# A macaron block on one core: the shared expert taken for two groups of tokens at once, in the two halves of the array's rows

## The chip, the core and the metric

The kernel runs on one core of one Trainium2 chip. The core has a matrix engine (TensorE, "PE" in the profile, with its weight loads shown apart as "PEld"), a vector engine (VectorE, "DVE"), a scalar engine (ScalarE, "ACT"), a general engine (GpSimd, "POOL") and an engine that issues most transfers (SyncE, "SP"). Matrix products are written to PSUM, a small memory of eight banks; one bank holds 128 rows of 512 numbers in float32. VectorE and ScalarE read results out of PSUM; GpSimd works on the larger on-chip memory, SBUF, alone. Each engine runs its own list of instructions in order, and engines wait for each other by semaphores.

The metric is the time of the kernel on the device in microseconds (us), as the median of several runs.

## What is computed

The input x is 8 sequences of 1024 tokens of width 128, all in float32. Three layers follow one another, each on a normalised x (mean and variance over the width of 128):

```python
x = x + 0.5 * ffn(layernorm(x))
x = x + attention(layernorm(x))     # one head of width 128, rotary positions, causal
x = x + 0.5 * ffn(layernorm(x))     # the same weights again
```

The feed-forward layer is a mixture of 16 experts of 64 hidden units, of which each token uses 4, and one shared expert of 64 hidden units that every token uses:

```python
scores = sigmoid(xt @ gate_w.T)                  # 16 scores per token
_, idx = top_k(scores + gate_b, 4)               # the 4 best experts
w = 2.5 * scores[idx] / sum(scores[idx])         # their weights, 0 for the others
y = sum over e of  w[e] * (silu(xt @ gate[e].T) * (xt @ up[e].T)) @ down[e].T
y = y + (silu(xt @ gate_sh.T) * (xt @ up_sh.T)) @ down_sh.T
```

## The kernel before

**Groups and slots.** A feed-forward layer is done in groups of 512 tokens (half a sequence); over the two layers there are 32 groups, numbered p = 0 to 31, in one order that lets attention of the sequences between the layers be filled in. The kernel computes all 16 experts for all tokens: their 1024 hidden units are 8 blocks of 128. A group has an "up" half, slots U0 to U8, and a "down" half, slots D0 to D8. In `up(k)` (line 278) TensorE makes two products of 128x512, gate and up, for block k into two PSUM banks (banks 1 and 0 for even k, 3 and 2 for odd k); ScalarE applies silu to the gate (line 286) and VectorE multiplies (line 288). In `weigh(k)` (line 290) GpSimd multiplies the block by the tokens' expert weights, which were spread over the partitions by a round trip through DRAM (`spread`, line 248). In `down(k)` (line 294) TensorE sums the eight blocks' products in bank 0. After each of these steps, `run(p, slot)` issues whatever other work has been given to that slot.

**The shared expert.** It has 64 gate units and 64 up units, so one product of 128x512 makes both halves (`up_shared_a`, line 267, into bank 5). `up_shared_b` applies silu to the gate half (line 275) and multiplies it by the up half (line 276) into rows 64 to 127 of a tile whose rows 0 to 63 are zero (`shared`, lines 129 to 133; the weights `wsd` have zeros in the same rows). A ninth product, `down(8)`, then adds it to bank 0 as a full product of 128 rows, of which half are zero. It closes the sum; VectorE copies the result out of bank 0 (`yT`, line 306). The shared product of a group is issued at its start, ahead of slot U0, and `down(8)` ahead of slot D8.

**The other work, by slot.** A list `jobs` is filled by hand-written tables of slots. For group p, the work that prepares it is placed in the groups before it: normalisation (`norm_a`, `norm_b`), the transposition into `hT` (`turn`, line 189), the scores of the 16 experts (`route_a`, `route_b`, `score`), the choice of the best four (`top_a` and `top_b` in slot D8, `top_c` in U1, all VectorE), and `spread` in U3. `add` (line 323) turns the previous group's `yT` back and adds it to x in slot U3. Attention is done in queries of 128 tokens: `scores`, `exp`, `turn` (transposing the probabilities), `attend` (line 435). Each group carries two or three queries; their slots are at lines 483 to 487: the first one's `attend` is in D7, the second's first `turn` is in D8, its second in U0 and its `attend` in U2, and a third's turns are in U3 and U4. The projections for a new sequence (`project`, line 361, banks 5 and 4) are in U3 and U4.

**Spare banks.** Everything that is neither up, down, shared, projection nor scores takes its PSUM bank from `other_bank()` (line 73): banks 6 and 7 in turn. An instruction that takes such a bank waits until the last user's result has been read out of it.

**One matmul, two instructions.** A float32 product appears in the profile as two weight loads and two matmuls (two passes), so a line called 256 times shows 512 matmuls. The routing product (line 197) is split over four blocks of 32 columns of the array (`tile_position=(0, j * SW)`), four tiles of 128 tokens each.

**The opening.** For group 0 all preparation runs ahead of the loop: `turn`, `route_a`, `up_shared_a`, `route_b`, `score` and the choice of experts (lines 569 to 580). Slot U1 of group 0 begins with its `spread` (lines 582 to 585), then statistics, a load of x, and the loads of the attention's weights. Groups 1 and 2 have their own tables of places (lines 526 to 531).

Of the kernel before, what the change touches and what calls it, by code (L numbers as in the profile page):

```python
# [26 lines left out]
def kernel(  # L27
# [43 lines left out]
    spare = [0]  # L71

    def other_bank():
        spare[0] += 1
        return bank(6 + spare[0] % 2)
# [51 lines left out]
    nc.gpsimd.memset(wsd[:I, :], 0.0)  # L127
    nc.sync.dma_start(out=wsd[I:, :], in_=w_sh_down)
    shared = []
    for n in range(2):  # L130
        sh = const.tile([P, W], F32, name=f"shared{n}")
        nc.gpsimd.memset(sh[:I, :], 0.0)
        shared.append(sh)
# [43 lines left out]
    class Group:  # L177
# [89 lines left out]
        def up_shared_a(self):  # L267
            self.hidT = big.tile([P, NP, W], F32, tag="hidT", name=f"hidT_{self.nm}")
            self.sh = shared[self.n % 2]
            nc.tensor.matmul(bank(5), ws, self.hT, start=True, stop=True)  # L270

        def up_shared_b(self):
            s_ps = bank(5)
            ss = work.tile([P, W], F32, tag="sg", name=f"ss_{self.nm}")
            nc.scalar.activation(ss[I:, :], s_ps[:I, :], AF.Silu)  # L275
            nc.vector.tensor_tensor(self.sh[I:, :], s_ps[I:, :], ss[I:, :], ALU.mult)

        def up(self, k):

            nm = f"{self.nm}_{k}"  # L280
            units = slice(k * P, (k + 1) * P)
            g_ps, u_ps = bank(2 * (k % 2) + 1), bank(2 * (k % 2))
            nc.tensor.matmul(g_ps, wg[:, units], self.hT, start=True, stop=True)  # L283
            nc.tensor.matmul(u_ps, wu[:, units], self.hT, start=True, stop=True)  # L284
# [3 lines left out]
            nc.vector.tensor_tensor(hid, u_ps, sg, ALU.mult)  # L288
# [5 lines left out]
        def down(self, k):  # L294
            if k == 0:
                self.y = bank(0)
            w, h = (wd[:, k, :], self.hidT[:, k, :]) if k < NP else (wsd, self.sh)
            nc.tensor.matmul(self.y, w, h, start=(k == 0), stop=(k == NP))  # L298
            if k == NP:
                self.yT = work.tile([P, W], F32, tag="yT", name=f"yT_{self.nm}", bufs=2)  # L300
                if self.n == NPER - 1:
                    H = W // 2
                    nc.scalar.copy(self.yT[:, :H], self.y[:, :H])
                    nc.vector.tensor_copy(self.yT[:, H:], self.y[:, H:])
                else:
                    nc.vector.tensor_copy(self.yT, self.y)
# [16 lines left out]
        def add(self):  # L323
# [8 lines left out]
            if self.layer == 1:  # L332
                nc.sync.dma_start(
                    out=out[self.b].rearrange("(t p) d -> p t d", p=P)[:, tiles, :], in_=xg
                )

# [161 lines left out]
    for b in range(B):  # L498
# [5 lines left out]
        else:  # L504
            p0, p1 = st - 2, st - 1
            places = ("D0", "D3", "D5", "D8", "U1", "U3", "U4", "U6")
# [9 lines left out]
        at(st, "U3", lambda h=h: h.project(0, 1))  # L516
        at(st, "U4", lambda h=h: h.project(1, 1))
# [3 lines left out]
    for p, gr in enumerate(groups):  # L521
# [36 lines left out]
    at(0, "U7", lambda: stats("f0_1", 1, range(GT)))  # L558
# [6 lines left out]
    def run(p, slot):  # L565
# [9 lines left out]
    gr.up_shared_a()  # L575
# [6 lines left out]
    jobs[0, "U1"] = [  # L582
        lambda: gr0.spread(4), lambda: stats("f0_0", 0, range(GT, NT)), groups[1].norm_a,
        lambda: load_x(1, 1), load_attention,
    ] + jobs.get((0, "U1"), [])
    gr0 = gr
    for p, gr in enumerate(groups):
        if p > 0:
            gr.up_shared_a()
        gr.up_shared_b()  # L590
        run(p, "U0")
        for k in range(NP):
            gr.up(k)
            if p == 0 and k == 0:
                run(p, f"U{k + 1}")
                gr.weigh(k)
# [3 lines left out]
        for k in range(NP + 1):  # L600
            gr.down(k)
# [76 lines left out]
```

## Time and profile before

| What | Value |
|---|---|
| Median of 3 runs | 1007.22 us (1007.2 to 1007.79) |
| The profiled execution | 1008.41 us, of which 1006.6 us from the first to the last instruction |
| TensorE matmul busy | 988.0 us (98% of the span), 3590 instructions |
| VectorE busy | 663.9 us (66%) |
| ScalarE busy | 427.4 us (42%) |
| GpSimd busy | 451.8 us (45%) |
| Granted TensorE clock, mean | 0.998 of full speed |
| Shared expert's product up (line 270) | 32 products, 32.8 us busy |
| Shared expert's product down (line 298, `wsd`) | 32 products, 33.0 us busy |

The profile is of one execution. Busy time of TensorE is from the start of a matmul to its modelled end, and consecutive matmuls overlap; so what a product costs is read from the distance between its start and the next one's start. The idle time before an instruction and what ended it are given in brackets in the profile. A wait of the matrix engine is often shown at its weight load, which waits on the semaphore, and only in part at the matmul that follows it.

### The profile page before, as it was taken

What the parts mean: (1) busy time and instruction counts of PE and PEld (TensorE: products, weight loads), DVE (VectorE), ACT (ScalarE), POOL (GpSimd) and SP (SyncE); (2) the same over time, 40 slices, a digit from 0 to 9 for tenths busy, and PEclk for the clock granted to TensorE, in tenths of its full rate; (3) what the DMA queues carried; (4) which work ended last, traced back from release to release, by engine and by line L of the source; (5) the groups of instructions that cost most, each with busy time, mean ns of one, the idle gap of its engine ahead of it and who ended that gap; (6) DMA issues with size and microseconds to landing.
All of it is one profiled execution on the core that took longest, in us unless ns stands there. A gap on an engine that the chain in (4) does not pass through costs nothing.

```text
span 1006.6 us, 11516 instructions
## 1 busy us (share of the span) xinstructions
PE 988.0 (98%) x3590; PEld 516.4 (51%) x3590; DVE 663.9 (66%) x2034; ACT 427.4 (42%) x767; POOL 451.8 (45%) x382
## 2 busy tenths in 40 slices
PE   8999999999999999999999999999999999999998
PEld 5444445554555555545554555545554555455443
DVE  5766877668766667666767656776667757665542
ACT  3334435443544444443544444444444444343321
POOL 2445556244633464234634455234653355322434
PEclk9999999999999999999999999999999999999999
DMA  5645343044303532145403452134422243224440
GB/s 164 167 106 105 86 85 84 3 105 85 85 13 83 117 85 51 35 95 117 86 15 76 90 117 68 29 74 96 95 53 59 60 95 87 47 59 95 96 96 21
DMA packets 56830, 80.23 MB, mean 80 GB/s; under 512 B 3584, under 2 KB 23360, under 8 KB 56640
## 3 DMA queue, kind: packets, MB, share of 16 engines
q1 hardware_dynamic: 55488, 78.23, 34.7%
q10 hardware_dynamic: 1280, 1.26, 0.4%
q8 instruction: 28, 0.46, 0.2%
q14 instruction: 34, 0.28, 0.1%
HBM read 74.24 MB, written 5.24 MB: 79 GB/s over the span
## 4 chain that ended last, share of the span: by engine, by line
PE 89%; DVE 7%; issue 2%; ACT 1%; POOL 0%; ACTq 0%; POOLq 0%; DVEq 0%
PE psum L298 24%; PE psum L283 19%; PE psum L284 19%; PE psum L400 6%; PE psum L439 6%; PE psum L427 3%; PE psum L367 3%; PE psum L270 2%; PE psum L172 2%; DVE hidT L288 2%; PE psum L381 1%; DVE sel L237 1%; PE psum L197 1%; PE psum L328 1%; PE psum L139 1%
## 5 line engine op out<-in xcount | busy, mean ns | idle before, releaser
L292 POOL TENSOR_TENSOR hidT<-hidT,cb 128x512 f32<-128x512 f32 x256 | 323.8, 1271 | 515.7 <-DVE hidT L288 484.1
L284 PE MATMUL psum<-hT,wu 128*128 128x512 f32 x512 | 261.5, 592 | 0.6 <-DVE hidT L288 0.6
L283 PE MATMUL psum<-hT,wg 128*128 128x512 f32 x512 | 261.8, 593 | 0.0
L286 ACT ACTIVATE sg<-psum 128x512 f32<-128x512 f32 x256 | 152.7, 597 | 229.4 <-PE psum L283 216.5
L298 PE MATMUL psum<-hidT,wd 128*128 128x512 f32 x512 | 247.5, 601 | 0.0
L288 DVE TENSOR_TENSOR hidT<-psum,sg 128x512 f32<-128x512 f32 x256 | 175.4, 686 | 96.8 <-PE psum L284 93.8
L284 PEld LDWEIGHTS psum<-hT,wu 128*128 128x128 f32 x512 | 97.2, 190 | 123.4 <-issue 103.0
L298 PEld LDWEIGHTS psum<-hidT,wd 128*128 128x128 f32 x512 | 90.1, 191 | 80.9 <-issue 74.1
L283 PEld LDWEIGHTS psum<-hT,wg 128*128 128x128 f32 x512 | 88.5, 191 | 64.2 <-issue 61.6
L439 PEld LDWEIGHTS psum<-v,prT 128*128 128x128 f32 x576 | 74.4, 192 | 30.6 <-issue 26.3
L431 ACT COPY prT<-psum 128x512 f32<-128x512 f32 (+2 forms) x64 | 32.4, 506 | 108.1 <-PE psum L427 107.4
L439 PE MATMUL psum<-v,prT 128*128 128x128 f32 x576 | 74.6, 275 | 0.0
L400 PE MATMUL psum<-k,q 128*128 128x512 f32 (+2 forms) x192 | 72.4, 486 | 0.0
L443 DVE SCALAR_TENSOR_TENSOR x<-psum,rl,x 128x128 f32<-128x128 f32 x64 | 22.1, 346 | 68.3 <-PE psum L439 38.9
L163 DVE TENSOR_SCALAR xn_f<-x,mv_f,rs_f 128x128 f32<-128x128 f32 x128 | 64.9, 567 | 1.2 <-POOL rs_f L156 1.2
L427 PEld LDWEIGHTS psum<-ident,pr 128*128 128x128 f32 x288 | 36.7, 141 | 50.2 <-issue 34.2
L400 PEld LDWEIGHTS psum<-k,q 128*128 128x128 f32 x192 | 36.5, 190 | 45.9 <-issue 45.2
L406 DVE TENSOR_REDUCE top<-psum 128x1 f32<-128x128 f32 (+3 forms) x64 | 48.5, 758 | 2.2
L427 PE MATMUL psum<-ident,pr 128*128 128x128 f32 x288 | 47.4, 274 | 1.9 <-DVE x L331 1.9
L411 ACT ACTIVATE pr<-psum,top 128x128 f32<-128x128 f32 (+3 forms) x64 | 47.7, 746 | 0.3
L404 DVE TENSOR_TENSOR psum<-psum,causal 128x128 f32<-128x128 f32 x64 | 19.0, 296 | 42.4 <-PE psum L400 42.0
L275 ACT ACT_TABLE_LOAD x31 | 39.8, 1283 | 8.9 <-PE psum L270 8.8
(88 smaller groups left out, 1001.2 us busy)
## 6 DMA issues: line engine op xcount, KB each, us to landing
cb<-cd SPq DMA_DIRECT2D x124, 512.0 KB, 8.3
x<-in_x SPq DMA_DIRECT2D x16, 256.0 KB, 10.3
out_x<-x SPq DMA_DIRECT2D x15, 256.0 KB, 2.4
cb<-cd SPq DMA_DIRECT2D x8, 256.0 KB, 5.2
cd<-cT SPq DMA_DIRECT2D x32, 32.0 KB, 1.8
cs<-in_rope SPq DMA_DIRECT2D x1, 1024.0 KB, 9.8
wg<-in_w_gate ACTq DMA_DIRECT2D x2, 256.0 KB, 6.6
wu<-in_w_up ACTq DMA_DIRECT2D x2, 256.0 KB, 6.0
```

Source lines behind the costliest of these rows:

```text
L163: nc.vector.tensor_scalar(xn[:, j, :], xs[b][:, t, :], mvs[key][:, t, 0:1], rstd[:, j : j + 1], ALU.subtract, ALU.mult,)
L283: nc.tensor.matmul(g_ps, wg[:, units], self.hT, start=True, stop=True)
L284: nc.tensor.matmul(u_ps, wu[:, units], self.hT, start=True, stop=True)
L286: nc.scalar.activation(sg, g_ps, AF.Silu)
L288: nc.vector.tensor_tensor(hid, u_ps, sg, ALU.mult)
L292: nc.gpsimd.tensor_tensor(hid, hid, self.cb[:, k, :], ALU.mult)
L298: nc.tensor.matmul(self.y, w, h, start=(k == 0), stop=(k == NP))
L400: nc.tensor.matmul(s[:, c:e], h.q[:, i * P : width], h.k[:, c:e], start=True, stop=True)
L406: nc.vector.tensor_reduce(top, s[:, :width], AX.X, ALU.max)
L411: nc.scalar.activation(self.pr[:, : self.width], self.s[:, : self.width], AF.Exp, bias=self.top, scale=SCALE, accum_out=self.h.rl[:, self. ...
L427: nc.tensor.transpose(tp[:, j, :], self.pr[:, (k + j) * P : (k + j + 1) * P], ident)
L439: nc.tensor.matmul(o, self.prT[:, j, :], self.h.v[:, j, :], start=(j == 0), stop=(j == i))
```

## The change

**Two groups in one.** The shared expert is no longer part of a group. A new class `Shared` takes two groups, p and p + 1 with p even. Its `up` is at the start of the even group: two products of 128x512, one for each group, into banks 5 and 4; then, for each group, silu on ScalarE and a product on VectorE, whose result goes to rows 0 to 63 of one tile for the first group and to rows 64 to 127 for the second. Its `down`, in slot U2, makes four products of 64 rows and 256 columns: two column halves, and in each the first group in the array's rows 0 to 63 and the second in rows 64 to 127 (`tile_position=(n * I, 0)`), into banks 5 and 4. ScalarE copies both results into tiles `ys`. There are no zeros left in the tiles; `wsd` holds the weights twice, once in each half of the rows.

**The end of a group.** `down` has eight products, and a new method `close` takes the place of the copy: VectorE adds bank 0 and `ys` into `yT`. For the last group it does so in two halves, both on VectorE (before: one half on ScalarE, one on VectorE).

**A third spare bank.** From after `down(0)` until the jobs of slot D8, bank 1 is put at the front of the list of spare banks.

**Places.** The projections move from U3 and U4 to U4 and U5. In the opening, group 0's first gate product takes the place of its shared product, its `spread` and what goes with it move from U1 to U2, the shared products of groups 0 and 1 are in slots D0 and D3 of group 0, group 2 gets the table of the later groups, and statistics move from U7 to U4.

```diff
-    spare = [0]
+    spare = [6, 7]
     def other_bank():
-        spare[0] += 1
-        return bank(6 + spare[0] % 2)
+        spare.append(spare.pop(0))
+        return bank(spare[-1])
...
-    nc.gpsimd.memset(wsd[:I, :], 0.0)
-    nc.sync.dma_start(out=wsd[I:, :], in_=w_sh_down)
-    shared = []
     for n in range(2):
-        sh = const.tile([P, W], F32, name=f"shared{n}")
-        nc.gpsimd.memset(sh[:I, :], 0.0)
-        shared.append(sh)
+        nc.sync.dma_start(out=wsd[n * I : (n + 1) * I, :], in_=w_sh_down)
...
         def down(self, k):
             if k == 0:
                 self.y = bank(0)
-            w, h = (wd[:, k, :], self.hidT[:, k, :]) if k < NP else (wsd, self.sh)
-            nc.tensor.matmul(self.y, w, h, start=(k == 0), stop=(k == NP))
...
+            nc.tensor.matmul(
+                self.y, wd[:, k, :], self.hidT[:, k, :], start=(k == 0), stop=(k == NP - 1)
+            )
+
+        def close(self):
+            self.yT = work.tile([P, W], F32, tag="yT", name=f"yT_{self.nm}", bufs=2)
+            halves = [slice(0, W)]
+            if self.n == NPER - 1:
+                halves = [slice(0, W // 2), slice(W // 2, W)]
+            for c in halves:
+                nc.vector.tensor_tensor(self.yT[:, c], self.y[:, c], self.ys[:, c], ALU.add)
...
+    class Shared:
+        def __init__(self, pair):
+            self.pair = pair
+
+        def up(self):
+            self.h = work.tile([P, W], F32, tag="sh", name=f"sh_{self.pair[0].nm}", bufs=1)
+            for n, gr in enumerate(self.pair):
+                nc.tensor.matmul(bank(5 - n), ws, gr.hT, start=True, stop=True)
+            for n, gr in enumerate(self.pair):
+                s_ps = bank(5 - n)
+                ss = work.tile([P, W], F32, tag="sg", name=f"ss_{gr.nm}")
+                nc.scalar.activation(ss[I:, :], s_ps[:I, :], AF.Silu)
+                nc.vector.tensor_tensor(
+                    self.h[n * I : (n + 1) * I, :], s_ps[I:, :], ss[I:, :], ALU.mult
+                )
+
+        def down(self):
+            H = W // 2
+            for c in (slice(0, H), slice(H, W)):
+                for n in range(2):
+                    rows = slice(n * I, (n + 1) * I)
+                    nc.tensor.matmul(
+                        bank(5 - n)[:, c], wsd[rows, :], self.h[rows, c], start=True, stop=True,
+                        tile_position=(n * I, 0),
+                    )
+            for n, gr in enumerate(self.pair):
+                gr.ys = work.tile([P, W], F32, tag="ys", name=f"ys_{gr.nm}", bufs=2)
+                nc.scalar.copy(gr.ys, bank(5 - n))
...
-            places = ("D0", "D3", "D5", "D8", "U1", "U3", "U4", "U6")
+            places = ("D0", "D3", "D5", "D8", "U1", "U4", "U5", "U6")
...
-        at(st, "U3", lambda h=h: h.project(0, 1))
-        at(st, "U4", lambda h=h: h.project(1, 1))
+        at(st, "U4", lambda h=h: h.project(0, 1))
+        at(st, "U5", lambda h=h: h.project(1, 1))
...
-        elif p == 2:
-            places = [(0, s) for s in ("D0", "D3", "D5", "D6", "D7", "D8", "D8", "D8")]
-            places += [(p - 1, "U1"), (p - 1, "U3")]
...
+        if p % 2 == 0:
+            pair = Shared(groups[p : p + 2])
+            if p == 0:
+                at(0, "D0", pair.up)
+                at(0, "D3", pair.down)
+            else:
+                jobs[p, "U0"] = [pair.up] + jobs.get((p, "U0"), [])
+                at(p, "U2", pair.down)
...
-    at(0, "U7", lambda: stats("f0_1", 1, range(GT)))
+    at(0, "U4", lambda: stats("f0_1", 1, range(GT)))
...
-    gr.up_shared_a()
+    gr.gate(0)
...
-    jobs[0, "U1"] = [
+    jobs[0, "U2"] = [
         lambda: gr0.spread(4), lambda: stats("f0_0", 0, range(GT, NT)), groups[1].norm_a,
-        lambda: load_x(1, 1), load_attention,
-    ] + jobs.get((0, "U1"), [])
+        lambda: load_x(1, 1), load_attention, lambda: gr0.weigh(0),
+    ] + jobs.get((0, "U2"), [])
...
         for k in range(NP + 1):
-            gr.down(k)
+            if k < NP:
+                gr.down(k)
+            else:
+                gr.close()
+            if k == 0:
+                spare.insert(0, 1)
+            elif k == NP:
+                spare.remove(1)
             run(p, f"D{k}")
```

More of the change, by code (lines that the diff above doesn't have):

```diff
@@ L265, in spread, with gate @@
                     )
[L267 to L276, printed above, removed]
+        def gate(self, k):
+            units = slice(k * P, (k + 1) * P)
+            nc.tensor.matmul(
+                bank(2 * (k % 2) + 1), wg[:, units], self.hT, start=True, stop=True
+            )
         def up(self, k):
+            if k == 0:
+                self.hidT = big.tile([P, NP, W], F32, tag="hidT", name=f"hidT_{self.nm}")
             nm = f"{self.nm}_{k}"
@@ L282, in up @@
             g_ps, u_ps = bank(2 * (k % 2) + 1), bank(2 * (k % 2))
-            nc.tensor.matmul(g_ps, wg[:, units], self.hT, start=True, stop=True)
+            if self.n > 0 or k > 0:
+                self.gate(k)
             nc.tensor.matmul(u_ps, wu[:, units], self.hT, start=True, stop=True)
@@ L296, in down @@
                 self.y = bank(0)
-            w, h = (wd[:, k, :], self.hidT[:, k, :]) if k < NP else (wsd, self.sh)
[L298 to L306, printed above, removed]
+            nc.tensor.matmul(
[8 more added lines that the diff above has]
+                nc.vector.tensor_tensor(self.yT[:, c], self.y[:, c], self.ys[:, c], ALU.add)
         def add_last(self):
@@ L335, in add @@
                 )
+    class Shared:
[17 more added lines that the diff above has]
+                    rows = slice(n * I, (n + 1) * I)
+                    nc.tensor.matmul(
+                        bank(5 - n)[:, c], wsd[rows, :], self.h[rows, c], start=True, stop=True,
+                        tile_position=(n * I, 0),
+                    )
+            for n, gr in enumerate(self.pair):
+                gr.ys = work.tile([P, W], F32, tag="ys", name=f"ys_{gr.nm}", bufs=2)
+                nc.scalar.copy(gr.ys, bank(5 - n))
     class Heads:
@@ L580 @@
     gr.top_c()
-    jobs[0, "U1"] = [
+    jobs[0, "U2"] = [
         lambda: gr0.spread(4), lambda: stats("f0_0", 0, range(GT, NT)), groups[1].norm_a,
-        lambda: load_x(1, 1), load_attention,
-    ] + jobs.get((0, "U1"), [])
+        lambda: load_x(1, 1), load_attention, lambda: gr0.weigh(0),
+    ] + jobs.get((0, "U2"), [])
     gr0 = gr
     for p, gr in enumerate(groups):
-        if p > 0:
-            gr.up_shared_a()
-        gr.up_shared_b()
         run(p, "U0")
@@ L593 @@
             gr.up(k)
-            if p == 0 and k == 0:
+            if p == 0 and k < 2:
                 run(p, f"U{k + 1}")
-                gr.weigh(k)
+                if k == 1:
+                    gr.weigh(k)
             else:
@@ L600 @@
         for k in range(NP + 1):
-            gr.down(k)
+            if k < NP:
+                gr.down(k)
+            else:
+                gr.close()
+            if k == 0:
+                spare.insert(0, 1)
+            elif k == NP:
+                spare.remove(1)
             run(p, f"D{k}")
```

## The prediction

> **What bounds the kernel now.** I read the chain that ended last first, then the matrix engine's groups and waits, then the timeline at a group's end, engine by engine.
>
> ```profile
> PE 89%; DVE 7%; issue 2%; ACT 1%; POOL 0%; ACTq 0%; POOLq 0%; DVEq 0%
> ```
>
> TensorE sets the time; what is taken from it counts, unless something else then becomes late. The shared expert's products, in the groups by form:
>
> ```profile
> L298 PE MATMUL psum<-shared,wsd 128*128 128x512 f32 x64 | 33.0, 597 | 0.0
> L270 PE MATMUL psum<-hT,ws 128*128 128x512 f32 x64 | 32.8, 595 | 0.0
> ```
>
> Busy time overlaps the next product; in the timeline below starts are 0.86 us apart, so 32 products down take 27.5 us, and as many go up. What TensorE waits for (its waits, longest first):
>
> ```profile
> PE psum L328 <- DVE x L443: 3.9, 6, 1.0
> PE psum L252 <- DVE comb L243: 2.7, 3, 2.3
> PE psum L427 <- DVE x L331: 1.9, 5, 0.4
> PE psum L252 <- DVE x L443: 1.7, 3, 0.8
> ```
>
> All are VectorE, and the first, third and fourth are spare banks not yet read out. The places matter: the end of group 12 and the start of 13 on TensorE:
>
> ```profile
> 418.06 1.02 PE L298 MATMUL psum<-shared,wsd 128*128 128x512 f32 x2
> 418.92 0.27 PE L427 MATMUL psum<-ident,pr 128*128 128x128 f32 x1
> 419.02 1.02 PE L270 MATMUL psum<-hT,ws 128*128 128x512 f32 x2
> 419.89 1.02 PE L283 MATMUL psum<-hT,wg 128*128 128x512 f32 x2
> 420.74 1.02 PE L284 MATMUL psum<-hT,wu 128*128 128x512 f32 x2
> ...
> 425.26 0.60 PE L328 MATMUL psum<-ident,yT 128*128 128x128 f32 x4
> 426.63 0.30 PE L252 MATMUL psum<-ident,comb 128*64 128x128 f32 x1 [0.77 <-DVE x L443]
> 426.77 0.59 PE L283 MATMUL psum<-hT,wg 128*128 128x512 f32 x1
> ```
>
> and on VectorE:
>
> ```profile
> 419.12 0.69 DVE L306 COPY yT<-psum 128x512 f32<-128x512 f32 x1
> ...
> 422.15 0.69 DVE L276 TENSOR_TENSOR shared<-psum,ss 64x512 f32<-64x512 f32 x1
> 422.88 0.69 DVE L288 TENSOR_TENSOR hidT<-psum,sg 128x512 f32<-128x512 f32 x1
> ...
> 426.24 0.34 DVE L443 SCALAR_TENSOR_TENSOR x<-psum,rl,x 128x128 f32<-128x128 f32 x1
> ```
>
> Between them VectorE has no gap: the copy, the choice of experts, the shared product, two up products and the choice's second part end only at 426.58, and TensorE, arriving at 425.70, waits. Here both engines are full; elsewhere TensorE is full alone.
>
> **What the Trainium skill says.** "TensorEngine Tiling (Array Packing)", Key Properties: tiles of the array work independently, and changing the tiling mode drains the array. The routing product, four column tiles in eight passes, agrees with both:
>
> ```profile
> 118.38 1.02 PE L298 MATMUL psum<-hidT,wd 128*128 128x512 f32 x2
> 119.33 0.43 PE L197 MATMUL psum<-hT,gw 128*32 128x128 f32 x8
> 119.69 1.12 PE L298 MATMUL psum<-hidT,wd 128*128 128x512 f32 x2
> ```
>
> The product before would be followed at 119.24. Eight passes of 128 columns at 0.107 would take 0.86 us in a row; they take 0.45 with the switch, and the product after is longer by 0.10. Two rounds of four are 0.21, so switching costs 0.34 us. The same page's Gotcha 1: row tiles must write to different banks; the change uses 5 and 4. "TensorE: Matmul & The Clock Gate", Measured speedup, has four row tiles at 3.07 times; no row tile is in this trace. "PSUM — Partial Sum Buffer", PSUM bank collisions: two engines may not be in one bank at once; the waits above are that rule at work.
>
> **The change, part by part.** T is the time at which TensorE has done slot D7.
>
> *Removed and added on TensorE.* Per pair, two products down go (1.72 us); four of 64 rows and 256 columns come, 0.43 us each (a scores product of 256 columns is followed after 0.43). If the two halves of the array stream together: 0.86 + 0.34 for the switch = 1.20 us. If passes are taken strictly in order, two per tile, neighbours overlap in five rounds of 0.215: 1.41. If not at all: 1.72 + 0.34 = 2.06. I take 1.20, since column tiles do overlap. Naive gain: 16 x 0.52 = 8.3 us. The products up stay 32, but both at the even group's start.
>
> *Odd groups.* TensorE loses 1.72 us ahead of slot U3 (one product down, one up); VectorE only its shared product, 0.70. Redo group 13. The closing addition costs what the copy cost (0.69) and starts at the same T + 1.1, because VectorE was at the preceding attention result until T + 1.0. So bank 0 is free at T + 1.83 and the first up product, reachable at T + 0.97, waits 0.86. The attention result of U2 ends at 8.52 - 0.70 = T + 7.84, `spread` starts at 7.90 and the fourth gate at T + 8.03; before, it was 8.71. Gain 0.68, not 1.72. The same sum for each odd group:
> - 7, 13, 17, 21, 27 (VectorE sets the end): 0.7 each, 21 0.9; 3.6 us.
> - 5, 9, 11, 15, 19, 23, 25, 29, which have more transposes, attention products or a projection there as cover: 1.15 to 1.6; 10.6 us.
> - 3: 0, since VectorE is later still (copy at T + 2.37); 31: 1.6, as nothing is chosen there.
> Sum 15.8 us of 25.8.
>
> *Even groups.* Ahead of U3: minus one product down, plus one up, plus 1.20: 1.20 us more, in 15 groups 18.0. VectorE gets 0.70 more. Relief: TensorE comes later to the waits of `add` or `spread`, so they shrink by 0.33 to 0.40 in groups 2, 4, 10, 14, 20, 24, 28, 30 (3.0 us). Projections after `add` let its result (line 331) be read out earlier; the wait of L427 on it in U4, 0.54 us by start times, goes in 6, 8, 12, 18, 26 (2.7 us). The products down in U2 need the second shared result, VectorE at about T + 5.55; TensorE comes at 5.5 to 7, so it is nearly covered.
>
> *The third bank and D8.* Without `down(8)`, the transposes of D8 follow D7 at once. With three spare banks, where the first query has at most four tiles, they find a free bank. Otherwise the rotation hands them the bank of D7's `attend`, read out at T + 0.44 to 0.50: 0.5 us of new wait. It counts in even groups 6, 12, 16, 22, 26: 2.5 us; in 10 and 20 it is hidden by a later wait, and odd groups have it in my sums. In D itself no wait for a bank is seen before, so there is nothing to gain.
>
> *ScalarE* has 32 copies more, 0.6 us each, at U2 to U3, where it has gaps over 1 us; the first silu's table load (1.28 us) now waits for the first gate product in odd groups. Silu at T + 3.8 is ahead of VectorE at 4.1: no cost. GpSimd drops two clears (0.5 us each) before anything waits for it; SP issues one weight transfer more, before x's second half is needed.
>
> *Opening.* Before, TensorE waits 2.4 us at 14.9 for the choice of experts, and 1.6 us at 35.1 for group 2's normalised x, after which it runs slowly until 40.5. Afterwards two more products stand ahead of the first wait in the shared one's place (0.86 us gained), and group 2's preparation, earlier, together with 2.9 us of shared work put ahead of D4 leaves about 0.65 of the second. The move of `spread` to U2 carries its nine transfers and the loads of x and of attention's weights on SP's queue, but they wait for the choice of experts (VectorE, 14.85) either way, so they start when they did. VectorE's statistics at U4 and GpSimd's `pow` between the weighings take back some. Up to group 1's fourth gate I get 3.2 us, by far my least certain term (0 to 6).
>
> *Tail.* One product down less after the last pair: 0.86 us; the two half additions follow each other as the copies did (ScalarE's and VectorE's were already one after the other, 1002.07 and 1002.48).
>
> Sum: 18.0 - 3.0 - 2.7 + 2.5 = +14.8 in even groups; -15.8 in odd; -3.2; -0.9: **-5.1 us** on a profiled span of 1006.6, to 1001.5. The profiled execution took 1008.4, 1.8 more than its span; the median of runs is 1.2 below that execution, so 1007.2 - 5.1 = 1002.1.
>
> **Rivals.**
> - *TensorE gets most of it*: VectorE's chain is shorter than I think, for instance since the line 237 product (1.26 us here, 0.22 in the opening) is slowed by GpSimd's first weighing and may fall elsewhere. Then 8.3 + 5.7 of waits gone + 3 = 17: 990 to 998. Against it: the chain has no gap.
> - *Row tiles don't overlap*: 2.06 us. Place: U2 of each even group; 0.86 x 16 = 13.8 more, about 2 absorbed by waits at `add`: 1002 + 12 = 1014, **slower**. It decides when the four products pass 1.2 + 5.1/14 = 1.55 us. For it: no row tile in the trace. Against it: the column tiles.
> - *In between*: passes chained (1.41, +3.4 us), or a missed wait of 0.2 us per group: 1005 to 1009.
> - *It doesn't do what it says*: the third bank is such a part; it changes waits by under 3 us in either direction.
>
> **How the numbers follow.** As worked out, 998.5 to 1005: 0.52. Most of it: 0.17. In between: 0.15. No overlap: 0.13; other, slower: 0.03. A measurement here can tell about 0.2%, 2 us: faster is below 1005.2. Faster 0.51 + 0.17 + 0.05 = 0.73; same 0.01 + 0.09 = 0.10, rounded up to 0.11; slower 0.16. Leaving out half of the fast rival and the end of the slow one: 995 to 1011.
>
> **What would show it.** The four row-tile products start within 0.9 us and the next gate comes 1.2 us after their first. In odd groups the first up product waits for the closing addition, and `spread` for line 443. L427's wait on L331 is gone. D8's first transpose waits for line 443 where the first query is long. A wait of TensorE in D4 of group 0 below 1 us. I am wrong if the row tiles run one after the other, or if odd groups gain their whole 1.72.

## The result, and the profile after

The changed kernel takes 1008.94 us (median of 22 runs, 1008.24 to 1010.65), the kernel before 1007.2 us (22 runs, 1006.63 to 1009.27). The ratio is 1.0015, with a 95% interval of 1.0009 to 1.0022: within the 0.2% that a measurement here can tell, and if anything slower. Forecast were 1002.1 us and a faster kernel. The time lies in the range (995 to 1011) and inside the rival "in between" (1005 to 1009), which had 0.15.

The profiled execution took 1008.44 us with a span of 1006.7, against 1008.41 and 1006.6 before. So by these two spans the change is worth +0.1 us, where -5.1 was worked out. The medians differ by 1.6 us more than that, and this lies in which executions were traced. The changed kernel's was a typical one: its 22 spans have a median of 1006.9. The one before was long for its kernel, whose spans in the later sessions have medians of 1005.3 to 1005.9. In that trace the clock granted to TensorE is half of full speed from 36.9 to 40.3 us, after the wait that ends at 35.1, and a product there takes twice its 1.02 us:

```profile
37.77 2.08 PE L298 MATMUL psum<-hidT,wd 128*128 128x512 f32 x2
```

By starts (from one product's start to the next one's) the products in this stretch cost 1.7 us more than elsewhere. The changed kernel's trace has no such stretch. What a typical execution before looks like at this place is not shown.

The chain that ended last, in shares of the span by engine, after the change:

```profile
PE 91%; DVE 5%; ACT 1%; POOL 1%; DMA 1%; issue 1%; SPq 0%; DVEq 0%; POOLq 0%
```

TensorE has more of the chain and VectorE less. The shared products by form (total busy us, mean ns):

```profile
L342 PE MATMUL psum<-hT,ws 128*128 128x512 f32 x64 | 30.1, 593 | 0.0
L356 PE MATMUL psum<-sh,wsd 64*128 64x256 f32 x128 | 18.1, 402 | 0.0
```

The products down fell from 33.0 to 18.1 us of busy time. What TensorE waits for now (total us, times, longest):

```profile
PE psum L454 <- DVE x L470: 5.2, 13, 0.4
PE psum L248 <- DVE comb L239: 2.0, 2, 1.4
PE psum L248 <- ACT prT L458: 1.7, 7, 0.2
PE psum L248 <- DVE x L470: 1.7, 3, 0.7
...
PE psum L278 <- DVE yT L302: 1.2, 1, 1.2
```

The first and the last did not stand in the list before, and the third stood there with a single wait of 0.2, in group 28. The first is D8's transpose, which waits for the bank of D7's attention result. In the third, `spread` (line 248) waits for ScalarE. The wait of U4's turn for `add` (5 times, 1.9 us) is gone, and `add`'s own wait fell from 3.9 to 0.6 us. Where it is seen best is group 12, on TensorE:

```profile
380.74 0.66 PE L454 MATMUL psum<-ident,pr 128*128 128x128 f32 x4 [0.41 <-DVE x L470]
381.23 1.88 PE L342 MATMUL psum<-hT,ws 128*128 128x512 f32 x4
...
386.61 1.50 PE L466 MATMUL psum<-v,prT 128*128 128x128 f32 x12
388.04 1.13 PE L356 MATMUL psum<-sh,wsd 64*128 64x256 f32 x8
389.10 1.12 PE L265 MATMUL psum<-hT,wg 128*128 128x512 f32 x2
390.06 1.02 PE L278 MATMUL psum<-hT,wu 128*128 128x512 f32 x2
390.92 0.60 PE L454 MATMUL psum<-ident,pr 128*128 128x128 f32 x4
391.36 0.60 PE L324 MATMUL psum<-ident,yT 128*128 128x128 f32 x4
392.20 0.30 PE L248 MATMUL psum<-ident,comb 128*64 128x128 f32 x1 [0.24 <-ACT prT L458]
```

and the same stretch on ScalarE:

```profile
389.20 1.07 ACT L362 COPY ys<-psum 128x512 f32<-128x512 f32 x2 [2.66 <-PE psum L356]
390.26 0.60 ACT L280 ACTIVATE sg<-psum 128x512 f32<-128x512 f32 x1
391.56 0.59 ACT L458 COPY prT<-psum 128x512 f32<-128x512 f32 x1 [0.70 <-PE psum L454]
392.54 0.26 ACT L250 COPY cT<-psum 64x128 f32<-64x128 f32 x1 [0.39 <-PE psum L248]
```

The third query's first turn (line 454, at 390.92) fills a spare bank. ScalarE copies it out from 391.56 to 392.15. `add` takes the other spare bank, and `spread` needs the first one again. It could start at 391.80 and starts at 392.20. ScalarE is not behind: it was idle for 0.70 us before this copy, and the copies of the shared sums (line 362) were over at 390.27. The same place before the change:

```profile
390.82 0.60 PE L427 MATMUL psum<-ident,pr 128*128 128x128 f32 x4
391.25 1.02 PE L367 MATMUL psum<-hT_a,wqkv 128*128 128x512 f32 x2
392.11 0.60 PE L328 MATMUL psum<-ident,yT 128*128 128x128 f32 x4
392.55 0.27 PE L252 MATMUL psum<-ident,comb 128*64 128x128 f32 x1
```

There a projection of 0.86 us (line 367) stood between the turn and `add`, and the copy was hidden under it.

Set against each other by the start of the eighth product down of each group, the two traces give this account (us):

| Part | Worked out | Measured |
|---|---|---|
| Odd groups 3 to 31 | -15.8 | -15.9 |
| Even groups 2 to 30 | +14.8 | +18.8 |
| Opening, up to group 1's fourth gate | -3.2 | -2.8 |
| Group 1's second half | 0 | +0.6 |
| Tail | -0.9 | -0.7 |
| Sum | -5.1 | +0.1 |

The half-clock stretch lies in the opening, and its 1.7 us are part of the 2.8 there; the rows of the odd and even groups are untouched by it.

### The profile page after: what moved, and what is told of

Read it like the earlier page. It is cut to its first block, busy times and chain, and to the rows that moved or that the text cites. A ratio compares the mean times of both kernels' runs of the same rounds, so it can differ in the third digit from the quotient of the medians.

```text
span 1006.7 us, 11656 instructions
## 1 busy us (share of the span) xinstructions
PE 985.8 (98%) x3654; PEld 515.9 (51%) x3654; DVE 670.5 (67%) x2035; ACT 444.2 (44%) x798; POOL 450.7 (45%) x379
## 3 DMA queue, kind: packets, MB, share of 16 engines
q10 hardware_dynamic: 1280, 1.26, 0.4%
## 4 chain that ended last, share of the span: by engine, by line
PE 91%; DVE 5%; ACT 1%; POOL 1%; DMA 1%; issue 1%; SPq 0%; DVEq 0%; POOLq 0%
PE psum L291 21%; PE psum L265 20%; PE psum L278 20%; PE psum L466 6%; PE psum L427 6%; PE psum L454 3%; PE psum L342 3%; PE psum L394 3%; PE psum L168 2%; PE psum L356 2%; PE psum L408 1%; PE psum L193 1%; PE psum L324 1%; DVE x L470 1%; DMA cb<-cd 1%
## 5 line engine op out<-in xcount | busy, mean ns | idle before, releaser
L427 PE MATMUL psum<-k,q 128*128 128x512 f32 (+2 forms) x192 | 72.4, 486 | 0.0
L159 DVE TENSOR_SCALAR xn_f<-x,mv_f,rs_f 128x128 f32<-128x128 f32 x128 | 68.5, 595 | 1.9 <-POOL rs_f L152 1.7
L427 PEld LDWEIGHTS psum<-k,q 128*128 128x128 f32 x192 | 36.5, 190 | 45.9 <-issue 44.7
L152 POOL TENSOR_TENSOR rs_f<-rs_f,neg_half 128x4 f32<-128x4 f32 x32 | 32.4, 1013 | 16.8 <-DVE rs_f L151 16.3
```

What stands on the lines that cost most here:

```text
L159: nc.vector.tensor_scalar(xn[:, j, :], xs[b][:, t, :], mvs[key][:, t, 0:1], rstd[:, j : j + 1], ALU.subtract, ALU.mult,)
L427: nc.tensor.matmul(s[:, c:e], h.q[:, i * P : width], h.k[:, c:e], start=True, stop=True)
```

## Experiments

The theory after the result: TensorE does the saved products in fact, but the even groups pay more than worked out, because the projection that left slot U3 had been the cover for ScalarE's copy of the third query's turn. Beside it stand rivals: that ScalarE is late because of its 32 new copies; that the row tiles do not overlap or depend on their order; that the third bank brings the waits at D8. All runs below, unless said otherwise, are timed beside the kernel before (medians there of 1007.06 to 1007.67 us); ratios are to it.

### The two new waits taken away, each alone and both

"Route first": in slot D7, the routing scores' transposition (line 202) and its exponential come ahead of the attention product, so that D8's transposes take other banks.

```diff
+            ahead = [f for f, place in zip(steps, places) if place[1] == "D7"]
             for f, place in zip(steps, places):
-                at(*place, f)
+                if place[1] != "D7":
+                    at(*place, f)
+            if ahead:
+                jobs[p - 2, "D7"] = ahead + jobs.get((p - 2, "D7"), [])
```

> The changed kernel with one edit: in slot D7 the routing transposition stands ahead of the first query's attention products, so that the transposition of slot D8 gets the routing's bank and not the attention's. Theory A (the change's gain is lost at single waits for a bank, each tied to a place in the order): the 13 waits of 0.57 us ahead of the D8 transposition go, 7.4 us in all, of which about 3 come back at the first up product of odd groups; 4 us faster than the changed kernel, ratio to the kernel before 0.997 to 0.998. Theory B (VectorE's chain at the boundary is full, and a wait taken away at one place comes back at the next): within 1.5 us of the changed kernel, ratio 1.000 to 1.002.

"Spread in U5": `spread` leaves slot U3, where it had met the bank that ScalarE still reads.

```diff
-            places += [(p - 1, "U1"), (p - 1, "U3")]
+            places += [(p - 1, "U1"), (p - 1, "U5")]
```

> The changed kernel with one edit: the spreading of the expert weights (a transposition, a copy, nine transfers) is in slot U5 in place of U3, for groups 2 to 31. Theory A: the wait for a bank ahead of it in U3 goes, about 0.4 us in the even groups with a third query and 0.6 to 0.9 in the odd groups where line 470 ended it; 6 us faster than the changed kernel, ratio about 0.996. Theory B: VectorE is late for the up products anyway, TensorE then waits at the gate or up product of block 2 or 3; within 2 us of the changed kernel, ratio 1.000 to 1.002.

Both edits together:

> The changed kernel with both edits: routing ahead of attention in D7, spreading in U5. Theory A: the two gains add, 9 to 11 us faster than the changed kernel, ratio 0.991 to 0.993. Theory B: within 2 us of the changed kernel.

| Kernel | Median, us | Ratio, 95% interval | Span, us |
|---|---|---|---|
| changed | 1008.94 | 1.0015 (1.0009 to 1.0022) | 1006.7 |
| + route first | 1005.31 | 0.9978 (0.9970 to 0.9987) | 1002.9 |
| + spread in U5 | 1002.83 | 0.9955 (0.9942 to 0.9968) | 1001.0 |
| + both | 999.37 | 0.9920 (0.9907 to 0.9933) | 997.5 |

Theory A holds in all three. By starts, the waits between lines 202 and 454 (7.4 us in 13 groups) are gone in the first, those between `add` and `spread` (6.7 us in 16 groups) in the second. A part comes back: in the first, VectorE's closing addition is later for TensorE, and the wait of the first up product for it grows from 2.4 to 5.0 us. With both edits this is the head of the list of waits:

```profile
PE psum L278 <- DVE yT L302: 3.9, 6, 1.7
```

### The closing addition earlier

On top of both edits, `close` is issued right after the eighth product down instead of after slot D7's jobs.

```diff
         for k in range(NP + 1):
             if k < NP:
                 gr.down(k)
-            else:
+            if k == NP - 1:
                 gr.close()
```

> The changed kernel with the routing product ahead of the attention product in slot D7, the spreading product in slot U5, and now also VectorE's closing addition issued straight after the eighth product down instead of after slot D7. Theory A (in odd groups the first up product waits for bank 0 only because VectorE does D7's attention result first): the kernel with the first two edits has 5.4 us of that wait left in 8 groups; VectorE now closes the sum while TensorE does D7's work, so most of it goes: 4 to 5 us faster than that kernel, ratio to the kernel before 0.987 to 0.989. Rival B (VectorE's chain as a whole is full in these groups, and the order on it decides nothing): the wait reappears at the attention result or at the third query's turn, ratio 0.991 to 0.993, as without this edit.

Measured: 995.17 us, ratio 0.9876 (0.9863 to 0.9889), span 992.6. That is 4.2 us faster than without it, as theory A had it. Group 13, in which VectorE set the end, on TensorE and VectorE:

```profile
411.70 1.95 PE L466 MATMUL psum<-v,prT 128*128 128x128 f32 x16
413.49 0.27 PE L454 MATMUL psum<-ident,pr 128*128 128x128 f32 x1
413.60 1.02 PE L265 MATMUL psum<-hT,wg 128*128 128x512 f32 x2
414.46 1.02 PE L278 MATMUL psum<-hT,wu 128*128 128x512 f32 x2
```

```profile
411.79 0.69 DVE L302 TENSOR_TENSOR yT<-psum,ys 128x512 f32<-128x512 f32 x1
413.69 0.35 DVE L470 SCALAR_TENSOR_TENSOR x<-psum,rl,x 128x128 f32<-128x128 f32 x1 [1.21 <-PE psum L466]
```

The sum is closed while TensorE does D7's attention product, and the first up product no longer waits. This version beats both kernels, by 12.5 us the one before. A further step on top of it, `add` in slot U4 instead of U3, gave nothing more:

> The changed kernel with the routing product first in D7, the spreading product in U5, the early closing addition, and also the addition to x in slot U4. It has only 1.0 us of waits left at the addition. Theory A (TensorE's own products now set its time): within 0.2% of the kernel with the early closing addition, ratio 0.986 to 0.989. Rival B (the later addition holds up x, and the normalised x of a later group becomes late): over 0.99.

995.28 us, ratio 0.9881 (0.9866 to 0.9896): the same, as theory A expected.

### What the change itself is worth

The same care given to the kernel before. First, `spread` in U5 alone (the same one-line edit):

> The kernel before with one edit: the spreading in U5 in place of U3. It tells whether the second edit is worth as much without the change. Theory A: the waits ahead of it in U3 in the kernel before (lines 328 and 252 on line 443 and on the choice of experts) are about 3 us for the spreading alone, so 2 to 3 us faster, ratio 0.997 to 0.998; the changed kernel with the same edit is then faster than this one by at least 1 us. Theory B: nothing changes, ratio 1.000.

Measured: 1000.89 us, ratio 0.9935 (0.9921 to 0.9949). That is 6.5 us, about twice what I had expected. The trace shows why: besides the waits at `spread` itself (3.5 us by starts in 7 groups), those of U4's turn for `add`'s result (2.7 us) went too, since `spread` no longer takes the bank in between. The other half of the expectation failed: the changed kernel with this edit is not 1 us faster than the old one with it, but 1.9 us slower (1002.83). Then `add` in U4 as well:

```diff
-        at(p + 1, "U3", gr.add)
+        at(p + 1, "U4", gr.add)
```

> The kernel BEFORE the change, with the spreading product in slot U5 and the addition to x in slot U4 instead of U3: the shared expert stays one full product per group. This asks what the change is worth once the old form has had the same care for its waits. Theory A (the 4.9 us that the addition waits in six groups for slot U2's attention result are a matter of places alone): 4 to 5 us faster than with the spreading product's move, ratio 0.988 to 0.990; the changed kernel with its own best places, 0.9876, is then hardly ahead, and what the change brings by itself is under 2 us. Rival B (VectorE's chain is full, and the wait moves to the third query's turn in U4): 0.992 to 0.994, and the change is worth about 6 us, close to the 0.45 us for each of 16 pairs that its products save.

Measured: 997.4 us, ratio 0.9909 (0.9896 to 0.9923), between the two expectations and nearer to A: 3.5 us faster than with the first edit, and the waits at `add` (4.9 us by starts) gone. What TensorE then still waits for in the old form:

```profile
PE psum L252 <- DVE comb L243: 2.3, 1, 2.3
PE psum L139 <- POOL ident masks.py:199: 1.5, 1, 1.5
PE psum L284 <- DVE hidT L288: 1.4, 3, 0.6
```

So with places tended on both sides the new form has 995.2 us and the old one 997.4. What the change brings by itself is about 2 us by medians, the least that a measurement here can tell, and 3.0 by spans (992.6 against 995.5). Neither form's places were searched to the end, so this holds for these two sets of places. Group by group, the new form's even groups cost 18.3 us more than the old form's, and its odd groups 20.2 less. The pairs are worth 1.9 us of the 3.0, the opening and the tail 1.1; the old form's trace has a half-clock stretch in its opening (15.9 to 19.3 us), the new one's has none. 15 pairs at 1.72 - 1.27 would be 6.8. Group 3 keeps back 1.4 of that, because VectorE is late for its up products. Most of what else is kept back is again in the bank rotation. In eight odd groups the transposes at D8 start late behind D7's attention result or a turn's copy, 0.2 to 0.5 us by the account of the groups, and in group 27 `add` waits once for 1.2:

```profile
860.22 0.66 PE L324 MATMUL psum<-ident,yT 128*128 128x128 f32 x4 [1.04 <-DVE x L470]
```

### The projections back in U3 and U4

```diff
-            places = ("D0", "D3", "D5", "D8", "U1", "U4", "U5", "U6")
+            places = ("D0", "D3", "D5", "D8", "U1", "U3", "U4", "U6")
...
-        at(st, "U4", lambda h=h: h.project(0, 1))
-        at(st, "U5", lambda h=h: h.project(1, 1))
+        at(st, "U3", lambda h=h: h.project(0, 1))
+        at(st, "U4", lambda h=h: h.project(1, 1))
```

> The changed kernel with the projections back in slots U3 and U4, as before the change; nothing else. Theory A (the projection that was moved out of U3 had hidden ScalarE's copy of the third query's turned probabilities, for which the spreading product now waits 0.40 us by starts in groups 6, 8, 12, 14, 18, 26, 28): in the groups that have a projection in U3 this wait goes, 2 to 2.5 us in all, and in return the turn in U4 waits again for the addition's result to be read out, 2.7 us: within 0.1% of the changed kernel, ratio to the kernel before 1.000 to 1.003, with the two waits seen to trade places. Rival B (ScalarE is late because it copies the shared sums, whatever stands in U3): the wait for ScalarE's copy stays in those groups and the U4 wait is added, 1.003 to 1.006.

Measured: 1008.79 us, ratio 1.0016 (1.0010 to 1.0023), span 1007.1. The two waits trade places, as theory A says. Group 12 again on TensorE:

```profile
390.85 0.60 PE L454 MATMUL psum<-ident,pr 128*128 128x128 f32 x4
391.28 1.02 PE L394 MATMUL psum<-hT_a,wqkv 128*128 128x512 f32 x2
392.14 0.60 PE L324 MATMUL psum<-ident,yT 128*128 128x128 f32 x4
392.58 0.27 PE L248 MATMUL psum<-ident,comb 128*64 128x128 f32 x1
...
394.95 0.55 PE L454 MATMUL psum<-ident,pr 128*128 128x128 f32 x3 [0.38 <-DVE x L327]
```

`spread` follows `add` at once in groups 6, 8, 12, 18 and 26; in 14 and 28, which have no projection in U3, it still waits 0.40 us. In exchange, U4's turn waits 0.54 us in the five. ScalarE's copies of the shared sums are there in this kernel too, so they are not what makes ScalarE late: rival B is out. By these waits the whole move of the projections was worth 2.7 - 2.0 = 0.7 us, not 2.7; the spans differ by 0.4, the medians by less than they can tell.

### The row tiles

"Same rows": both shared results go to rows 0 to 63 of one wider tile, and the four products down use the same half of the array.

```diff
-                    rows = slice(n * I, (n + 1) * I)
+                    cols = slice(n * W + c.start, n * W + c.stop)
                     nc.tensor.matmul(
-                        bank(5 - n)[:, c], wsd[rows, :], self.h[rows, c], start=True, stop=True,
-                        tile_position=(n * I, 0),
+                        bank(5 - n)[:, c], wsd[:I, :], self.h[:I, cols], start=True, stop=True,
+                        tile_position=(0, 0),
                     )
```

> The changed kernel with both groups' shared products down in the same 64 rows of the array, so that the four products of 64 rows and 256 columns can only follow one another; all else as in the changed kernel. Theory A (the two row tiles stream together, and that is why the block takes 1.27 us): the four products now take 4 x 0.43 = 1.72 us and the switch 0.34: 0.8 us more in each of 16 even groups, 12.8 us, less up to 2.8 us of waits at the spreading product that are then covered: 10 to 13 us slower than the changed kernel, ratio to the kernel before 1.011 to 1.014. Rival B (the tiles do not overlap, and the short block comes from the half-filled array alone): the same as the changed kernel, 1.001 to 1.002.

Measured: 1021.95 us, ratio 1.0144 (1.0131 to 1.0158), 13.0 us above the changed kernel: at the far end of theory A. Group 12's block:

```profile
392.55 1.99 PE L356 MATMUL psum<-sh,wsd 64*128 64x256 f32 x8
394.47 1.12 PE L265 MATMUL psum<-hT,wg 128*128 128x512 f32 x2
```

1.92 us from the first product to the gate, where the changed kernel has 1.06. The 0.86 us come 16 times, 13.8 us, and only group 0 gives some back, about 0.6 us: the wait of `spread` for ScalarE, in which I had seen a reserve, follows the turn and not the block, and stays (0.24 us before line 248, as above).

"Full width": no column halves, two products of 512 columns.

```diff
-            H = W // 2
-            for c in (slice(0, H), slice(H, W)):
+            for c in (slice(0, W),):
```

> The changed kernel with the two row tiles at their full width of 512 columns, without column halves: two products of 64 rows instead of four. Theory A (each row tile streams its own products, whatever their order in the list): the block takes the same 1.2 to 1.3 us, or a little less, as there are four weight loads fewer, ratio to the kernel before 1.001 to 1.002. Rival B (passes are taken strictly in the order of the list, two per product, and only neighbours of different rows overlap): first pass alone, one overlapped pair, last pass alone, 3 x 0.43 + 0.34 = 1.63 us, 0.36 us more in 16 groups, 5 us less what the wait at the spreading product gives back: 1.004 to 1.007.

Measured: 1008.89 us, ratio 1.0015 (1.0009 to 1.0022), the same as the changed kernel to the last digit shown. The block:

```profile
388.27 1.13 PE L355 MATMUL psum<-sh,wsd 64*128 64x512 f32 x4
389.33 1.12 PE L265 MATMUL psum<-hT,wg 128*128 128x512 f32 x2
```

1.06 us again. The instructions' records of this block show two first passes starting 6 ns apart and two second passes 7 ns apart. In the same rows passes of 256 columns follow one another after 0.22 us, so these pairs are one pass of each tile. The halves are not needed for the overlap.

### The third spare bank

```diff
-            if k == 0:
-                spare.insert(0, 1)
-            elif k == NP:
-                spare.remove(1)
```

> The changed kernel without the third spare bank: banks 6 and 7 in turn, as before. Theory A (the D8 wait of 0.57 us comes from the product down(8) that no longer stands between D7's attention result and D8's first transpose; the third bank spares it where the rotation is kind): it now stands in all groups with a query instead of 13, up to 13 x 0.57 = 7 us more, of which about half is given back at later waits: 2 to 5 us slower than the changed kernel, ratio to the kernel before 1.0035 to 1.0065. Rival B (the rotation of three is what brings the wait, since with two banks D8's transpose takes the bank that was free longest): the D8 waits go, and the time is 1 to 4 us below the changed kernel, 0.998 to 1.0005.

Measured: 1013.81 us, ratio 1.0064 (1.0050 to 1.0078), 4.9 us slower than the changed kernel. Its first wait:

```profile
PE psum L454 <- DVE x L470: 9.6, 26, 0.4
```

26 groups instead of 13: theory A. The wait comes with the removal of `down(8)`, which had stood between D7's attention result and D8's transposes. The third bank takes it away in half of the groups and is worth 4.9 us there, where the prediction gave it under 3.

### The opening

Group 2's old table of places and the statistics back in U7:

```diff
+        elif p == 2:
+            places = [(0, s) for s in ("D0", "D3", "D5", "D6", "D7", "D8", "D8", "D8")]
+            places += [(p - 1, "U1"), (p - 1, "U3")]
...
-    at(0, "U4", lambda: stats("f0_1", 1, range(GT)))
+    at(0, "U7", lambda: stats("f0_1", 1, range(GT)))
```

> The changed kernel with group 2's old table of places, and the statistics of the second sequence back in slot U7; the rest of the opening as changed. Theory A (the opening's gain of 2.8 us up to group 1's fourth gate comes in part from these two moves, which end the wait for group 2's normalised x): 1 to 2 us slower than the changed kernel, ratio to the kernel before 1.0025 to 1.0035. Rival B (the gain comes from the products that stand ahead of the first wait, and the 0.6 us lost in group 1's second half is these moves' price): the same or up to 0.6 us faster than the changed kernel, 1.000 to 1.002.

Measured: 1009.44 us, ratio 1.0023 (1.0013 to 1.0034). By medians this is 0.5 us more than the changed kernel, within the two intervals; by the two traced spans 1.7 us more (1008.4 against 1006.7), and all of it is there by the end of group 1. The traced execution was the longest of its eight; the median spans differ by 0.8. The wait in D4 of group 0 is back:

```profile
36.61 1.09 PE L168 MATMUL psum<-ident,xn_f 128*128 128x128 f32 x4 [1.25 <-DVE xn_f L159]
```

against 0.45 in the changed kernel. The direction is that of theory A; the size, between 0.5 and 1.7 us, stays open.

### The choice of experts elsewhere: a miss

Two kernels move the choice of experts (`top_a` to `top_c`) from D8 and U1 to U6, U7 and U8, and `spread` to D1: one of the changed kernel with route first and early close, one of the kernel before.

```diff
-            places = [(p - 2, s) for s in ("U5", "D1", "D4", "D5", "D7", "D7", "D8", "D8")]
-            places += [(p - 1, "U1"), (p - 1, "U3")]
+            places = [(p - 2, s) for s in ("U5", "D1", "D4", "D5", "D7", "D7")]
+            places += [(p - 1, s) for s in ("U6", "U7", "U8", "D1")]
```

> As the kernel with the early closing addition, but the choice of experts (its three parts on VectorE) moves from slots D8 and U1 to U6, U7 and U8 of the group before the one that needs it, and the spreading product to its slot D1. Theory A (VectorE's work at the groups' boundary, about 4.5 us in one go, is what is still late there once the closing addition is early): 1 to 3 us faster than with the early closing addition alone, ratio 0.985 to 0.987. Rival B (nothing of VectorE is late any more after the early closing addition): the same as that kernel within 0.1%.

> The kernel BEFORE the change, with the choice of experts in slots U6, U7 and U8 and the spreading product in slot D1, nothing else. Theory A (what limits both kernels beyond TensorE's own work is VectorE's choice of experts at the groups' boundary, and the change only shifted who waits for it): the waits of the kernel before at the spreading product (3.5 us), at the U4 turn (2.7) and part of those at the addition to x (3.9) go: 7 to 10 us, ratio 0.990 to 0.993. Then the change with its waits removed stands against this by the 8 us of products that it saves, less the D8 waits. Rival B (the gain of the spreading product's move was all there is): 0.9935, as with that move alone.

Measured: 1115.38 us, ratio 1.107 (1.1056 to 1.1085), and 1085.35 us, ratio 1.0793 (1.0761 to 1.0825). Both expectations missed by far. The first one's longest wait:

```profile
PE psum L248 <- DVE comb L239: 61.4, 24, 3.8
```

with 19.0 us more of `spread`'s waits put down to line 151, also VectorE; and one such place on TensorE, then the choice's end on VectorE:

```profile
452.51 1.88 PE L291 MATMUL psum<-hidT,wd 128*128 128x512 f32 x4
457.06 0.27 PE L248 MATMUL psum<-ident,comb 128*64 128x128 f32 x1 [2.67 <-DVE comb L239]
```

```profile
454.64 0.22 DVE L232 TENSOR_TENSOR sel<-rp,biased 128x64 f32<-128x64 f32 x1
454.89 1.25 DVE L233 TENSOR_TENSOR sel<-sel,sc 128x64 f32<-128x64 f32 x1
...
456.64 0.27 DVE L239 SCALAR_TENSOR_TENSOR comb<-sel,tot 128x64 f32<-128x64 f32 x1
```

I had asked only what is relieved at the groups' boundary, not when the choice would be ready in its new place: it ends on VectorE at 456.91, 2.7 us after TensorE could do `spread` (four passes of 0.43 after 452.51), since VectorE is behind TensorE by the last hidden product and the choice's third part alone takes 2.3 us. `spread` two slots after `top_c` is too near; in U3 or U5, two and four slots after U1, each slot has 1.7 us of gate and up products, while D0 and D1 have 0.86. What the move would give with `spread` later in the down half was not tried.

The waits are not the whole loss. The first kernel's span is 120 us over that with the early closing alone, and its mean granted clock is 0.972 instead of 1.000 of full speed. In 18 stretches of 3.4 us, each beginning during such a wait or up to 1.2 us after one, TensorE has half its clock: about 31 us, an estimate (half of 18 x 3.41). The second kernel has 9 of them, and a mean clock of 0.986.

## Why the prediction was wrong

- **The step that failed: "Projections after `add` let its result (line 331) be read out earlier; the wait of L427 on it in U4 ... goes in 6, 8, 12, 18, 26 (2.7 us)."** What goes did go, all of it. But the moved projection was entered as relief alone. It was also 0.86 us of cover between the third query's turn and `spread`, and without it the 0.59 us copy on ScalarE is late: 0.404 us in each of the five groups, 2.0 us. I had asked of ScalarE only whether its new copies find gaps ("no cost", right by itself), and not which of its old results TensorE would now come to earlier.
- **The relief at `add` and `spread` in eight even groups, 3.0 us:** 2.6 measured. In 2, 4, 10, 20, 24 and 30 it was 0.4 to 0.5, more than worked out. In 14 and 28 it was nothing. In 14 the wait at `add` shrank, and had been the cover of the same ScalarE copy, so `spread` took it over (0.40). In 28 `spread` had waited for that copy before already (0.40); the copy comes after a turn of TensorE's own, so a later TensorE does not shorten this wait. Same failure, second place.
- **The block at 1.20 us:** 1.27. The switch of 0.34 was taken from the column tiles; here it is 0.41: by the starts of group 12's block 0.10 ahead of it, 0.10 in its first round (0.32 instead of 0.215), 0.10 behind it and 0.11 in the gate that follows. 15 x 0.07 = 1.1 us.
- **D8's wait at 0.5 us:** 0.57 by starts, in the 13 groups. In the even ones that is 0.35 us more.
- These four make 2.0 + 0.4 + 1.1 + 0.35 = 3.9 of the 4.0 us by which the even groups were missed.
- **Opening:** 0.4 us less than worked out, even with the half-clock stretch gone, and group 1's second half lost 0.6 that was not foreseen: its D4 transposition waits for the normalised x (0.22 us in the profile at 58.2). The wait in D4 of group 0 is 0.45, below the 1 us that was named. Tail 0.2 short.
- **Right in the sum, in part by luck:** the odd groups, 15.9 us against 15.8. In 7, 13, 17, 21 and 27, where VectorE sets the end, TensorE gained 5.1 us instead of 3.6; in the eight with more cover 9.2 instead of 10.6. The two errors cancel. In group 13:

```profile
418.56 0.33 PE L454 MATMUL psum<-ident,pr 128*128 128x128 f32 x1 [0.41 <-DVE x L470]
425.61 0.30 PE L248 MATMUL psum<-ident,comb 128*64 128x128 f32 x1 [0.70 <-DVE x L470]
```

The new wait at D8 comes first (0.57 us by starts), so the first up product, which was to wait 0.86, waits 0.09; in the run with route first, without the wait at D8, it waits 0.76. `spread` waits for line 470 as foreseen, but starts 7.62 us after TensorE has done slot D7 (at 417.99) and not 7.90, as VectorE's chain is 0.28 us shorter than worked out. Of the eight others, 5, 15 and 25 have a second turn at D8 that waits 0.3 to 0.4 us for ScalarE's copy, the failed step's kind of wait again. What holds is that about 10 of TensorE's naive 25.8 us go to such waits.
- **Right:** the row tiles. The Trainium skill's statement that tiles work independently ("TensorEngine Tiling (Array Packing)", Key Properties) holds here for row tiles of float32 passes: 1.06 us to the next gate against 1.92 in the same rows. The rival without overlap fell with it, and so did the one of chained passes, by the run at full width.
- **The other rivals:** the range of "in between" held the time, at its upper edge; its "missed wait of 0.2 us per group" was one of 0.40 in seven groups, among the other misses. The fast rival (VectorE's chain shorter) is right by 0.28 us in group 13, but not for the reason it gave: the product of line 237 (now 233) takes 1.26 us as before.
- **The medians:** the forecast added the span's difference to the median before. The execution it was read from was 1.2 us longer than that median, and the one traced after 0.5 shorter than its own. The former had the half-clock stretch, which the prediction notes as "runs slowly until 40.5"; a saving read there need not be in the median. Whether the stretch is what made that execution long is not shown.

Why the edit moves so little is thus answered: the products are really saved, but odd groups give up 10 of 25.8 us to waits, most of them for VectorE, and the even groups pay 18.8. With waits removed on both sides, 2 to 3 us remain.

## What to carry to other kernels

When a step is moved away from between two others, cost the gap that it leaves as well as the relief that it brings: name each engine's result that was being read out underneath it (here a 0.59 us copy under a 0.86 us product). With banks handed out in turn, an added or removed user shifts every later wait; moving one step by two slots gave 6.5 us to the old kernel and 6.1 to the new one, more than the change of form is worth. So tend the places of the old form before crediting a new one.

## What the runs showed of the hardware

- Two row tiles of 64 rows, in float32 passes, run side by side at full rate: four products of 64x256 or two of 64x512 take the same 1.06 us to the next product's start, while the four in the same rows take 1.92.
- The order of the products in the kernel's text (tile A, tile B in column halves, or A whole and then B whole) made no difference: the tiles' passes started in pairs 6 to 7 ns apart in both.
- The switch of array form cost 0.41 us in all, a quarter of it each ahead of the tiles, in their first round, behind them and in the first full product after them, against the 0.34 us seen for column tiles.
- In five traces TensorE's granted clock fell to half in stretches of 3.4 us: one each in the kernel before and in its two versions with `spread` in U5, 9 and 18 in the two with the choice of experts moved. Each began during a wait of TensorE of 1.6 us or more, or up to 1.9 us after one. Not every such wait was followed by one: two other traces have a wait of 1.7 us and no stretch. Where TensorE was busy throughout, a stretch cost it 1.7 us by starts.
